# Layer 0's fp8 rounding in a two-layer Flamingo block: scaling on GpSimd, rounding in one ACT and two DVE operations

## The chip, the cores and the metric

The kernel runs on one core of one Trainium2 chip. A core has five engines that run side by side and meet at semaphores: TensorE (PE) for matrix products, VectorE (DVE), ScalarE (ACT) and GpSimd (POOL) for elementwise work, and SyncE (SP), which issues most DMAs. PE writes to PSUM; DVE and ACT read PSUM and SBUF; POOL reads SBUF. The time is that of one execution on the device in microseconds (us), the median of several; the profile is of one further execution.

## What is computed

Two layers of a gated block on x of 4 x 512 x 512, each a cross attention and a feed-forward part, each added to x with a factor tanh(g). The change touches the cross "attention" of layer 0 alone, which is a product of two quantized matrices:

```python
def quant_dequant_act_1x128(x):
    amax = jnp.max(jnp.abs(xb), axis=-1, keepdims=True)      # blocks of 128 along a row
    safe = jnp.maximum(amax, ACT_EPS)
    q = (xb * (FP8_MAX / safe)).astype(jnp.float8_e4m3fn)
    return (q.astype(jnp.float32) * (safe / FP8_MAX)).reshape(E, M, K)
...
xq = quant_dequant_act_1x128(x)           # x is layer-normed
wq = quant_dequant_weight_128x128(weight) # the same with 128 x 128 blocks; weight is the context
return jnp.einsum('emk,enk->emn', xq, wq)
```

So each block is scaled up to the range of an 8-bit float (3 bits of mantissa, the largest value 448), rounded to that format, and scaled down again. Behind it come layer 0's feed-forward part (weights rounded to -1, 0, 1; activations to 8-bit integers; two Gelu in a row), layer 1's attention with 16 heads, and layer 1's mixture of 8 experts.

## The kernel before

All of x lies in SBUF as 16 row tiles of 128 x 512 (`x_sb`). The work is staged: layer 0 (cross product and feed-forward woven together), then layer 1's attention, then the shared and the routed experts, which end with rows added to the output by scattering DMAs (L1481).

Layer 0 is written as steps `step(s)`, s from -7 to 14, each a slice through a pipeline over row tiles t: `cross_rows(s + 7)` normalizes, scales, rounds and scales back one row tile; `cross_product(s + 6)` turns the row tile before it on PE (L754), copies it from PSUM on ACT (L758), multiplies it with the quantized context (L761) and adds the result to `x_sb` on DVE (L768); `row_stats`, `row_norm` and `row_quant` (L797 to L846) prepare the tile for the feed-forward part; `hidden(s)` is its first product (L862) with two Gelu (L870, L877), `hidden_scales` takes the sum of squares on ACT (L885) and the largest value on DVE (L888, a 128x2048 reduction), `hidden_quant` rounds (L902), `down(s - 2)` is the second product (L912). The four contexts (`cross_context(b)`, each 128 x 4 x 512) are prepared in pieces between the steps: key and value products for layer 1 (L669, L681), the largest value of each 128 x 128 block (L696 to L711), and then, for each of the 4 chunks of 512 columns, the scaling up, the rounding and the scaling down. The two weights of the feed-forward part are summed (L637), and rounded on ACT and DVE (L659, L660), in steps -6 to -1.

The quantization before the change:

- Scaling up: for a context chunk, one DVE multiplication of 128x512 with the factors broadcast along 128 columns (L715); for a row tile, four ACT multiplications of 128x128, each with a factor for each row (L741).
- Rounding, `fp8_round`: four DVE operations on 128x512 (L136 to L141). The exponent of each value is cut out, scaled so that adding and subtracting it leaves 3 bits of mantissa, added, and subtracted.
- Scaling down: four ACT multiplications of 128x128 (L722 for a context, L747 for a row tile).

There are 16 context chunks and 16 row tiles, 32 units of 512 columns. POOL in layer 0 does only small operations: the power -1/2 of a few columns (L126, L804, L788), for which DVE waits behind each statistic. In layer 1 POOL adds the exponentials of the attention (L389, 128x1024) and a bias row to x (L1411, 128x512).

Each engine runs its instructions in its own order. That order isn't the source's: a scheduler arranges them by its own model of costs, except where the source pins them. Buffers come from rotating pools: row tiles `v` have 3 buffers, the rounding's scratch `e` has 2.

Of the kernel before, what the change touches and what calls it, by code (L numbers as in the profile page):

```python
# [10 lines left out]
F32 = mybir.dt.float32  # L11
BF16 = mybir.dt.bfloat16
I32 = mybir.dt.int32
I16 = mybir.dt.int16
U8 = mybir.dt.uint8
AF = mybir.ActivationFunctionType
ALU = mybir.AluOpType
# [3 lines left out]
P = 128  # L21
# [3 lines left out]
DC = D // P  # L25
# [18 lines left out]
FP8_MAX = 448.0  # L44
# [4 lines left out]
def flamingo_kernel(  # L49
# [22 lines left out]
    nc = tc.nc  # L72
# [9 lines left out]
    def acc(name):  # L82
        return ps_acc.tile([P, 512], F32, tag="acc", name=name)
# [45 lines left out]
    def layer_norm(dst, t, i, mv, rstd):  # L129
        nc.vector.tensor_scalar(  # L130
            dst, x_sb[:, t, :], mv[:, i, 0:1], rstd[:, i : i + 1], ALU.subtract, ALU.mult
        )

    def fp8_round(y, e):

        nc.vector.tensor_scalar(  # L136
            e.bitcast(I32), y.bitcast(I32), 0x7F800000, None, ALU.bitwise_and
        )
        nc.vector.tensor_scalar(e, e, 2.0**-6, 1.5 * 2.0**20, ALU.max, ALU.mult)
        nc.vector.tensor_tensor(y, y, e, ALU.add)  # L140
        nc.vector.tensor_tensor(y, y, e, ALU.subtract)  # L141

# [414 lines left out]
    with ExitStack() as l0:  # L559
# [9 lines left out]
        with ExitStack() as ph:  # L569
            other = ExitStack()  # L570
            cpool = other.enter_context(tc.tile_pool(name="cpool", bufs=3, side="right"))
            apool = other.enter_context(tc.tile_pool(name="apool", bufs=2, side="right"))
# [90 lines left out]
            def cross_context(b):  # L663


                c = state["ctx", b]
                k_ps = acc(f"k_ps_{b}")
                for dc in range(DC):
                    nc.tensor.matmul(  # L669
                        k_ps,  # L670
                        lhsT=wk_sb[:, dc, :],
                        rhs=c[:, dc, :],
                        start=dc == 0,
                        stop=dc == DC - 1,
                    )
                nc.scalar.copy(kT[:, b, :], k_ps)
                yield
                v_ps = acc(f"v_ps_{b}")
                for kc in range(TB):
                    for dc in range(DC):  # L680
                        nc.tensor.matmul(  # L681
                            v_ps[:, kc * P : (kc + 1) * P],
                            lhsT=c[:, dc, kc * P : (kc + 1) * P],
                            rhs=wv_sb[:, dc, :],
                            start=dc == 0,
                            stop=dc == DC - 1,
                        )
                nc.scalar.copy(
                    v_sb[:, b * TB : (b + 1) * TB, :], v_ps.rearrange("p (c n) -> p c n", c=TB)
                )  # L690
                yield
                cb = c.rearrange("p c (n q) -> p (c n) q", q=P)

                am = small.tile([P, 16], F32, tag="cam", name=f"cam_{b}", bufs=2)
                for ns in [slice(4 * dc, 4 * dc + 4) for dc in range(DC)] if b == 0 else [slice(16)]:
                    nc.vector.tensor_reduce(  # L696
                        am[:, ns], cb[:, ns, :], AX.X, ALU.max, apply_absolute_value=True
                    )
                tp = acc(f"tpm_{b}")
                nc.tensor.transpose(tp[:16, :P], am, ident)  # L700
                peak = small.tile([16, 1], F32, tag="cpeak", name=f"cpeak_{b}", bufs=2)
                nc.vector.tensor_reduce(peak, tp[:16, :P], AX.X, ALU.max)
                wide = small.tile([16, P], F32, tag="cwide", name=f"cwide_{b}", bufs=2)
                nc.vector.tensor_copy(wide, peak.to_broadcast([16, P]))
                nc.tensor.transpose(tp[:, P : P + 16], wide, ident[:16, :16])
                safe = small.tile([P, 16], F32, tag="csafe", name=f"csafe_{b}", bufs=2)
                nc.vector.tensor_scalar_max(safe, tp[:, P : P + 16], 1e-6)
                up = small.tile([P, 16], F32, tag="cup", name=f"cup_{b}", bufs=2)
                nc.vector.reciprocal(up, safe)
                nc.vector.tensor_scalar_mul(up, up, FP8_MAX)  # L710
                nc.vector.tensor_scalar_mul(safe, safe, 1.0 / FP8_MAX)  # L711
                yield
                for dc in range(DC):
                    ns = slice(dc * 4, dc * 4 + 4)
                    nc.vector.tensor_tensor(  # L715
                        cb[:, ns, :], cb[:, ns, :], up[:, ns].unsqueeze(2).to_broadcast([P, 4, P]),
                        ALU.mult,
                    )
                    e = apool.tile([P, 512], F32, tag="e", name=f"ce_{b}_{dc}")
                    fp8_round(c[:, dc, :], e)  # L720
                    for n in range(dc * 4, dc * 4 + 4):
                        nc.scalar.mul(cb[:, n, :], cb[:, n, :], safe[:, n : n + 1])  # L722
                    yield

            def cross_stats(b):
# [2 lines left out]
            def cross_rows(t):  # L728

                v = apool.tile([P, D], F32, tag="v", name=f"va_{t}", bufs=3)  # L730
                layer_norm(v, t, t % TB, *state["a", t // TB])
                vb = v.rearrange("p (c q) -> p c q", q=P)
                am = small.tile([P, DC], F32, tag="xam", name=f"xam_{t}")
                nc.vector.tensor_reduce(am, vb, AX.X, ALU.max, apply_absolute_value=True)
                nc.vector.tensor_scalar_max(am, am, 1e-4)
                up = small.tile([P, DC], F32, tag="xup", name=f"xup_{t}")
                nc.vector.reciprocal(up, am)
                nc.vector.tensor_scalar_mul(up, up, FP8_MAX)
                nc.vector.tensor_scalar_mul(am, am, 1.0 / FP8_MAX)
                for dc in range(DC):  # L740
                    nc.scalar.mul(vb[:, dc, :], vb[:, dc, :], up[:, dc : dc + 1])  # L741
                state["va", t] = v
                yield
                e = apool.tile([P, 512], F32, tag="e", name=f"xe_{t}")
                fp8_round(v, e)
                for dc in range(DC):
                    nc.scalar.mul(vb[:, dc, :], vb[:, dc, :], am[:, dc : dc + 1])  # L747
                yield

            def cross_product(t):  # L750
# [210 lines left out]
            with ExitStack() as first:  # L961
                stg = first.enter_context(tc.tile_pool(name="stg", bufs=4))
                ws = (w1T, w2T)
                wd = (w1q, w2q)
                load_batch(1)
                load_rows(1)
                load_weight(stg, 0, ws[0])
                load_batch(2)
                for b in range(2, B):
                    load_rows(b)  # L970
                go(cross_context(0), 7)
                cross_stats(0)

                def w(f, k, *cs):
                    return [lambda c=c: f(k, c, wd[k]) for c in cs]

                ctx1, ctx2 = cross_context(1), cross_context(2)
                step(-7)
                step(-6, [lambda: go(ctx1, 2)] + w(weight_sum, 0, 0, 1))
                step(-5, [lambda: go(ctx1, 2)] + w(weight_sum, 0, 2, 3))  # L980
                weight_mean(0)
                scales_left(0)
                step(-4, [lambda: go(ctx1, 3), lambda: cross_stats(1)] + w(weight_round, 0, 0, 1))
                load_weight(stg, 1, ws[1])
                step(-3, w(weight_round, 0, 2, 3) + w(weight_sum, 1, 0))
                load_batch(3)
                step(-2, [lambda: go(ctx2, 2)] + w(weight_sum, 1, 1, 2, 3))
                weight_mean(1)
                scales_left(1)
                step(-1, [lambda: go(ctx2, 2)] + w(weight_round, 1, 0, 1, 2, 3))  # L990
            hpool = ph.enter_context(tc.tile_pool(name="hpool", bufs=2))
            state["hpool"] = hpool
            step(0, [lambda: go(ctx2, 3), lambda: cross_stats(2)])
            ctx3 = cross_context(3)
            step(1)
            step(2, [lambda: go(ctx3, 3)])
# [292 lines left out]
    def rt(name, last=E, dtype=F32):  # L1289
        return dpool.tile([P, NT, last], dtype, name=name)  # L1290
# [17 lines left out]
    for n in range(2):  # L1308
        m, f = rt(f"m{n}", 1), rt(f"f{n}", 1)
# [285 lines left out]
```

## Time and profile before

| | us |
|---|---|
| median of 3 runs | 1294.44 (1291.94 to 1295.09) |
| the profiled execution | 1293.68, its span 1291.9 |
| PE busy over the span | 1188.1 (92%) |
| DVE busy | 610.2 (47%) |
| ACT busy | 511.2 (40%) |
| POOL busy | 410.7 (32%) |
| first and last Gelu on a product (L870) | start at 103.2 and 302.0 |
| first rounding (L136), last scaling down (L747) | start at 23.8 and 226.2 |

The granted clock of PE is 0.964 of full speed on average. In the profile a group is given by its line in the kernel, engine, operation, output and inputs with their shapes, count, busy time in us and the mean duration of one in ns; behind the bar stands the idle time of the engine just before these instructions and who ended it. Busy time of neighbours that overlap is counted once. In timelines a line has the start in us, the time of the merged pieces, and in brackets the idle time ahead of it.

### The profile page before, as it was taken

The numbers are of one execution on the slowest core, as the hardware profiler recorded it, in microseconds if no ns is written. First come the engines' busy times: TensorE is split into PE (matmuls) and PEld (weight loads), VectorE is DVE, ScalarE is ACT, GpSimd is POOL, SyncE is SP. The second block draws the span as 40 slices with busy tenths as digits, with TensorE's granted clock in tenths as the row PEclk, the third lists the DMA queues.
The fourth block names the chain that finished last, engine by engine and source line by source line (L and its number), as shares of the span: only waits on it lengthen the run. The fifth ranks groups of instructions, "written<-read, shape, count | busy, mean of one in ns | idle before, by whom it ended". The sixth has DMA issues, their size and how long they took to land. (4 is left out here: it accounts for less than half of the span.)

```text
span 1291.9 us, 14505 instructions
## 1 busy us (share of the span) xinstructions
PE 1188.1 (92%) x5354; PEld 550.2 (43%) x5354; DVE 610.2 (47%) x1160; ACT 511.2 (40%) x709; POOL 410.7 (32%) x408
## 2 busy tenths in 40 slices
PE   3776798899799999999999999999999999999995
PEld 1432343344233333333333554544335555555553
DVE  8789999688456666656654301331121111111110
ACT  4688898686355544444552110200001221211221
POOL 1000100101277877767686201136100111111111
PEclk8888999899899999999999889999999999999998
DMA  9230232335021211111003000027315886888782
GB/s 355 75 112 9 41 62 42 86 79 116 25 67 34 66 35 38 63 34 58 2 1 146 2 1 1 1 82 278 98 66 164 251 248 191 262 258 255 206 249 33
DMA packets 88753, 135.33 MB, mean 105 GB/s; under 512 B 52836, under 2 KB 54120, under 8 KB 84840
## 3 DMA queue, kind: packets, MB, share of 16 engines
q1 hardware_dynamic: 80936, 116.52, 28.3%
q0 software_dynamic: 7744, 17.86, 6.4%
q8 instruction: 43, 0.70, 0.2%
q14 instruction: 30, 0.25, 0.1%
HBM read 113.84 MB, written 32.32 MB: 113 GB/s over the span
## 5 line engine op out<-in xcount | busy, mean ns | idle before, releaser
L428 ACT ACTIVATE ex<-s,mbias,mk 128x1024 f32<-128x1024 f32 x128 | 147.2, 1200 | 140.7 <-PE s L239 140.7
L319 DVE TENSOR_REDUCE nmax<-s 128x2 f32<-128x1024 f32 x128 | 150.2, 1215 | 98.6 <-PE s L239 87.9
L1445 PE MATMUL gue<-w,xT 128*128 128x352 f32 x576 | 176.1, 459 | 0.0
L1481 POOL DMA_INDIRECT out_dram<-ye,row_i x36 | 55.5, 1541 | 320.1 <-ACT ye L1480 216.5
L389 POOL TENSOR_TENSOR part<-part,ex 128x1024 f32<-128x1024 f32 x62 | 144.6, 2354 | 16.3 <-PE sm L239 11.4
L1202 PE MATMUL gu<-xnT_d,w 128*128 128x512 f32 x320 | 144.0, 610 | 0.0
L1445 PEld LDWEIGHTS gue<-w,xT 128*128 128x128 f32 x576 | 109.2, 190 | 70.5 <-issue 16.9
L1465 DVE COPY hT<-tph_e 128x256 f32<-128x256 f32 x36 | 15.3, 425 | 255.2 <-PE tph_e L1463 255.2
L1472 PE MATMUL oe<-w,hT 128*128 128x512 f32 (+1 forms) x216 | 102.4, 610 | 3.8 <-ACT ye L1480 0.6
L1202 PEld LDWEIGHTS gu<-xnT_d,w 128*128 128x128 f32 x320 | 62.5, 196 | 78.3 <-issue 78.3
L761 PE MATMUL oa<-ctx,vTa 128*128 128x512 f32 x128 | 67.4, 675 | 18.9 <-ACT vTa L758 18.9
L1191 ACT ACTIVATE sg<-gu,sgb 128x512 f32<-128x512 f32 x20 | 13.7, 687 | 178.5 <-PE gu L1202 178.5
L389 POOL TENSOR_TENSOR part<-ex,ex 128x1024 f32<-128x1024 f32 x32 | 75.8, 2388 | 23.1 <-ACT ex L428 23.0
L912 PE MATMUL ob<-w2q,hqT 128*128 128x512 bf16 x256 | 64.9, 407 | 13.5 <-DVE hqT L838 10.3
L1453 ACT ACTIVATE sge<-gue 128x352 f32<-128x352 f32 x36 | 16.7, 463 | 151.5 <-PE gue L1445 151.5
L239 PE MATMUL s<-row_tables 10*128 10x512 bf16 (+1 forms) x512 | 67.5, 383 | 9.1 <-DVE nmax L319 5.7
L239 PE MATMUL s<-k,qT 32*128 32x512 f32 x512 | 72.2, 604 | 0.4 <-ACT qT L287 0.4
L239 PE MATMUL s<-qT,k 32*128 32x512 f32 x512 | 71.6, 598 | 0.0
L1192 DVE SCALAR_TENSOR_TENSOR hd<-gu,sub,sg 128x512 f32<-128x512 f32 x20 | 15.0, 751 | 117.9 <-ACT sg L1191 117.9
L239 PE MATMUL av<-ex,kv 128*32 128x512 f32 x512 | 69.2, 605 | 0.4 <-ACT ex L428 0.4
L239 PE MATMUL q_ps<-xnT,wq_sb 128*128 128x512 f32 (+1 forms) x156 | 68.8, 553 | 0.0
L239 PE MATMUL oc<-wo,attnT 128*128 128x512 f32 (+1 forms) x164 | 66.3, 525 | 0.0
(257 smaller groups left out, 1684.0 us busy)
## 6 DMA issues: line engine op xcount, KB each, us to landing
w<-in_e_w_dram SPq DMA_DIRECT2D x36, 1408.0 KB
w<-in_e_w_dram SPq DMA_DIRECT2D x36, 768.0 KB
slots<-row_tables SPq DMA_DIRECT2D x13, 771.0 KB
xr<-slots SPq DMA_DIRECT2D x36, 256.0 KB
stage<-in_w1T_dram SPq DMA_DIRECT2D x4, 1024.0 KB
stage<-in_w2T_dram SPq DMA_DIRECT2D x4, 1024.0 KB
k<-kv SPq DMA_DIRECT2D x64, 64.0 KB
out_dram<-x_sb SPq DMA_DIRECT2D x16, 256.0 KB
```

The lines of the kernel that those rows point to most:

```text
L239: tc.keep_in_program_order(nc.tensor.matmul(*args, **how))
L319: largest = nc.vector.tensor_reduce(nmax[:, i, 2 * j : 2 * j + 2], sc[j], AX.X, ALU.max, negate=True)
L389: nc.gpsimd.tensor_tensor(part[:, hs, :], old[:, hs, :], ex[:, hs, :], ALU.add)
L428: nc.scalar.activation(ex[:, 2 * j : 2 * j + 2, :], sc[j], AF.Exp, bias=mbias[:, b, kc : kc + 1], scale=mk[:, b, kc : kc + 1],)
L761: nc.tensor.matmul(o_ps[:, 0, :], lhsT=vT[:, dc, :], rhs=cq[:, dc, :], start=dc == 0, stop=dc == DC - 1,)
L912: nc.tensor.matmul(o_ps, lhsT=hqT[:, c, :], rhs=w2q[:, c * D : (c + 1) * D], start=c == 0, stop=c == IC - 1,)
L1202: nc.tensor.matmul(gu[:, m, :], lhsT=w[:, dc, c * P : (c + 1) * P], rhs=xnT[:, dc, b * S : (b + 1) * S], start=dc == 0, stop=dc == DC - 1,)
L1445: nc.tensor.matmul(gu[:, m, :I], lhsT=xT[:, dc, :], rhs=wt[:, dc, :], start=dc == 0, stop=dc == DC - 1,)
L1453: nc.scalar.activation(sg, gu[:, 0, :I], AF.Silu)
L1465: nc.vector.tensor_copy(hT[:, :2, :], tp[:, : 2 * P].rearrange("p (c q) -> p c q", q=P))
L1472: nc.tensor.matmul(o_ps[:, 0, :], lhsT=hT[:ni, c, :], rhs=dw[:ni, c, :], start=c == 0, stop=c == len(ICH) - 1,)
L1481: added = nc.gpsimd.indirect_dma_start(out=out, out_offset=bass.IndirectOffsetOnAxis(ap=row_i[:, j, 0:1].bitcast(I32), axis=0), in_=y, in_ ...
```

## The change

The scaling of a unit, up or down, is one POOL multiplication of 128x512 with the factors broadcast along 128 columns, for contexts and row tiles alike; the rounding is one ACT operation that writes the scaled absolute value as bf16, and two DVE operations with two tensors each, which leave the negated rounded value; the factor that scales back is negative accordingly. The scratch `e` becomes bf16.

```diff
+    def scale_blocks(y, by):
+        nc.gpsimd.tensor_tensor(y, y, by.unsqueeze(2).to_broadcast([P, 4, P]), ALU.mult)
+
     def fp8_round(y, e):
-        nc.vector.tensor_scalar(
-            e.bitcast(I32), y.bitcast(I32), 0x7F800000, None, ALU.bitwise_and
-        )
-        nc.vector.tensor_scalar(e, e, 2.0**-6, 1.5 * 2.0**20, ALU.max, ALU.mult)
-        nc.vector.tensor_tensor(y, y, e, ALU.add)
-        nc.vector.tensor_tensor(y, y, e, ALU.subtract)
+        least = 1.5 * 2.0**14
+        nc.scalar.activation(e, y, AF.Abs, scale=2.0**20)
+        nc.vector.scalar_tensor_tensor(y, e, least, y, ALU.max, ALU.add)
+        nc.vector.scalar_tensor_tensor(y, e, least, y, ALU.max, ALU.subtract)
...
-                nc.vector.tensor_scalar_mul(safe, safe, 1.0 / FP8_MAX)
+                nc.vector.tensor_scalar_mul(safe, safe, -1.0 / FP8_MAX)
...
-                    nc.vector.tensor_tensor(
-                        cb[:, ns, :], cb[:, ns, :], up[:, ns].unsqueeze(2).to_broadcast([P, 4, P]),
-                        ALU.mult,
-                    )
-                    e = apool.tile([P, 512], F32, tag="e", name=f"ce_{b}_{dc}")
+                    scale_blocks(cb[:, ns, :], up[:, ns])
+                    e = apool.tile([P, 512], BF16, tag="e", name=f"ce_{b}_{dc}")
                     fp8_round(c[:, dc, :], e)
-                    for n in range(dc * 4, dc * 4 + 4):
-                        nc.scalar.mul(cb[:, n, :], cb[:, n, :], safe[:, n : n + 1])
+                    scale_blocks(cb[:, ns, :], safe[:, ns])
...
-                nc.vector.tensor_scalar_mul(am, am, 1.0 / FP8_MAX)
-                for dc in range(DC):
-                    nc.scalar.mul(vb[:, dc, :], vb[:, dc, :], up[:, dc : dc + 1])
+                nc.vector.tensor_scalar_mul(am, am, -1.0 / FP8_MAX)
+                scale_blocks(vb, up)
...
-                e = apool.tile([P, 512], F32, tag="e", name=f"xe_{t}")
+                e = apool.tile([P, 512], BF16, tag="e", name=f"xe_{t}")
                 fp8_round(v, e)
-                for dc in range(DC):
-                    nc.scalar.mul(vb[:, dc, :], vb[:, dc, :], am[:, dc : dc + 1])
+                scale_blocks(vb, am)
```

## The prediction

> **What bounds the kernel now.** I read the busy slices first, then a table of stretches, then the groups and timelines of the first 240 us. The 40 slices are 32.3 us each.
>
> ```profile
> PE   3776798899799999999999999999999999999995
> ...
> DVE  8789999688456666656654301331121111111110
> ACT  4688898686355544444552110200001221211221
> POOL 1000100101277877767686201136100111111111
> ```
>
> Layer 0 is slices 1 to 10. There DVE is the fullest engine (7 to 9 tenths), ACT close behind, PE seldom full, and POOL almost empty. From slice 11 on PE is full. The chain of waits ends in the scatter of the last stage and goes back only to 1040 us, so it says nothing of layer 0; but attention needs layer 0's result and PE is full from there on, so what layer 0 gains or loses moves the end by as much.
>
> ```profile
> 20.00:40.00 20.00, 4.43 (x14) 2.14 (x13) 19.65 (x46) 16.05 (x34) 1.02 (x1) 0.57 0.74 278
> 40.00:60.00 20.00, 18.37 (x70) 10.35 (x70) 11.75 (x37) 9.76 (x19) 0.00 (x0) 0.92 0.03 7
> 60.00:80.00 20.00, 13.04 (x29) 5.47 (x28) 18.10 (x45) 19.03 (x40) 1.01 (x1) 0.83 0.71 256
> ...
> 100.00:120.00 20.00, 13.55 (x41) 5.85 (x40) 19.94 (x49) 17.46 (x38) 1.55 (x2) 0.83 0.07 14
> ...
> 160.00:180.00 20.00, 19.94 (x82) 9.03 (x81) 19.04 (x59) 20.00 (x35) 1.14 (x2) 1.00 0.33 62
> ```
>
> Columns: stretch, its length, busy time of PE, weight loads, DVE, ACT, POOL, the granted clock, DMA. DVE works over 18 of 20 us nearly everywhere; only 40 to 60 us waits on PE (18.37). Over 20 to 240 us DVE is busy 192.6 of 220 us (0.88), ACT 178. From 160 us PE and ACT are full too: a cheaper DVE would soon meet them there.
>
> **DVE, removed and added.** Per unit of 512 columns (16 context units, 16 row tiles) four roundings go, and per context unit the up-scaling.
>
> ```profile
> L140 DVE TENSOR_TENSOR va<-va,xe 128x512 f32<-128x512 f32 x16 | 10.8, 682 | 0.0
> ...
> L715 DVE TENSOR_TENSOR ctx<-ctx,cup 128x512 f32<-128x512 f32 x16 | 10.5, 683 | 0.0
> ...
> L139 DVE TENSOR_SCALAR xe<-xe 128x512 f32<-128x512 f32 x16 | 6.6, 418 | 0.0
> ...
> L212 DVE SCALAR_TENSOR_TENSOR ali<-ali,part,ali 128x512 f32<-128x512 bf16 x2 | 1.5, 748 | 0.0
> ```
>
> Neighbours overlap by some 0.08 us (in the timeline two L141 together take 1.28 us, two L139 0.75), so one costs 0.60 and 0.33 us of DVE. Removed: 32 x (0.33 + 0.33 + 0.60 + 0.60) + 16 x 0.60 = 69.1 us. Added: 64 scalar_tensor_tensor with a bf16 and an f32 input. L212 is that form, 748 ns, less 0.08: 64 x 0.67 = 42.9 us. Net -26.2 us.
>
> **ACT.** 192 scalings of 128x128 go; their three groups (L722, L741, L747) are busy 20.1 + 20.2 + 20.4 = 60.7 us. 32 Abs of 512 columns to bf16 come: L148, a bf16 cast of the same size, takes 618 ns, 0.52 with the overlap: 16.6 us. Net -44.1 us. No table load is added in the built order: the first and the Gelu table each stay in for all their Abs.
>
> **POOL.** 64 multiplications of 128x512 come. Its one row of that size is below. The second factor is broadcast along the inner axis, which no row shows; I take 1.27 us; the bounds are half of L389's 128x1024 (2.35 us), 1.18, and four of L414's 128x128 (0.456 us), 1.82, if each block of the broadcast were started anew. 64 x 1.27 = 81 us, onto the 19 us that POOL is busy up to 240 us. POOL is no bound by that alone. What counts is whom it stops.
>
> ```profile
> L1411 POOL TENSOR_TENSOR x_sb<-x_sb,sdb x16: 1260/1265/1498, 723.1 to 857.2; 128x512 f32<-128x512 f32 x16
> ```
> ```profile
> L130 DVE TENSOR_SCALAR vc<-x_sb,mv_c,rstd_c x16: 527/548/1993, 251.2 to 480.9; 128x512 f32<-128x512 f32 x16
> L130 DVE TENSOR_SCALAR vx<-x_sb,mv_d,rstd_d x16: 532/542/1490, 708.7 to 724.8; 128x512 f32<-128x512 f32 x16
> ```
> ```profile
> 368.85 1.98 DVE L130 TENSOR_SCALAR vc<-x_sb,mv_c,rstd_c 128x512 f32<-128x512 f32 x1 [2.49 <-PE tp L262]
> ```
> ```profile
> 368.20 4.84 POOL L389 TENSOR_TENSOR part<-ex,ex 128x1024 f32<-128x1024 f32 x2 [4.65 <-ACT ex L428]
> ```
> ```profile
> 822.18 1.26 DVE L1317 SCALAR_TENSOR_TENSOR prob<-hot,prob 128x128 f32<-128x128 f32 x1
> ```
> ```profile
> 822.02 1.26 POOL L1411 TENSOR_TENSOR x_sb<-x_sb,sdb 128x512 f32<-128x512 f32 x1 [2.18 <-DVE x_sb L1243]
> ```
>
> The reader is to see that DVE and POOL block each other. L130 takes 0.54 us alone, and up to 1.99 us when a POOL tensor_tensor is running: it starts at 368.85, the first of two POOL instructions (2.35 us each) ends at 370.55, and DVE ends 0.28 us later. A scalar_tensor_tensor with both inputs in SBUF does the same: 1.26 us instead of the 0.29 of its neighbours, ending 0.14 us behind POOL's end. DVE instructions that read PSUM, and reductions, run on (L319 stays at 1.2 us under POOL's 2.35). In layer 0 the changed kernel puts 64 POOL instructions beside just the kinds that are stopped: the 64 new two-input ones, L130 (0.54) and L838 (0.28 and 0.68).
>
> A DVE instruction that meets a 1.27 us POOL instruction at its start loses some 0.97 us (1.26 - 0.29), later in it less. In the built order of a row tile the up-scaling starts while DVE has the 2.28 us reduction L888 or the reduction L734 before it: nothing lost. The down-scaling starts right behind the second new instruction, and what follows on DVE is L130, L838 or the next unit's pair: nearly all of 0.97. In a context block four units are dense and the two engines alternate. So 0.5 us for each of the 64: +32 us of DVE; bounds 0 and 0.97 (0 and +62).
>
> The Trainium skill, "SBUF — State Buffer", section "Who interferes with whom", says that the two share one port pair as an exclusive lock held for the whole instruction, against 2-port modes and two SBUF inputs. By that sentence taken at its worst, each multiplication stopping DVE for its full length, DVE's change would be -26 + 81 = +55 us; the rows above show a DVE instruction slipping in between two queued POOL instructions, and the sum goes by them.
>
> **What else moves.** The rounding's chain becomes POOL (1.27), ACT (0.62), DVE, POOL, where it was DVE alone up to the last step. At the first context (22.6 us) nothing else is ready for DVE: it stands for 1.27 + 0.62 + 0.1 = +2 us (at the other three, rows in work cover it; bounds 0 and 8). Behind the multiplications stand POOL's 28 small pow instructions (L126, L788, L804), and DVE waits for these already now, 11.3 us in all (5.0 + 2.7 + 2.4 + 1.2). POOL is then busy some 0.4 of the time, so a pow finds on average 0.4 x 0.63 = 0.25 us ahead of it, 7 us in all; I put half on DVE's path: +3.5 (bounds 0 and 28 x 1.27 = 36). ACT's relief counts where ACT was last: between 56 and 82 us it is full, and 28 scalings (8.9 us) give way to some 7 Abs (3.6), so the second weight's sums come 5 us sooner, less the 2 to 3 us by which the first row tile is late: -3 (bounds 0 and -5.5). DMA issues on SP stand in the same order.
>
> **The sum.** DVE's own change, -26.2 + 32 = +5.8, counts at DVE's share 0.88: +5. With +2, +3.5 and -3 it is +7.5. The profiled execution took 1293.68 us (span 1291.9), 0.8 below the median of 1294.44. 1293.7 + 7.5 = 1301 us. With 0.25 us lost per POOL instruction, nothing else lost and ACT's full relief: (-26.2 + 16) x 0.88 - 5.5 = -14.5, 1279 us. With 0.75 us, and 4 and 7 for the waits: (-26.2 + 48) x 0.88 + 11 = +30, 1324 us.
>
> **Rivals.**
> 1. Faster: the scheduler's order lets the multiplications fall beside reductions and PSUM reads, which POOL does not stop. For it: L888 (36 us in all), L734, L815, L121 and L797 are a large part of DVE's time. Against it: the down-scaling starts right behind the pair. Place: DVE, 20 to 240 us; it decides below 0.35 us lost per multiplication (26.2 x 0.88 = 23.1, less 2.5 of the other terms, over 64 x 0.88), and over 0.3% faster needs 0.29. At 0.25 us and the middle of the other terms, -9 + 2.5 = -6.5 to -14.5: about 1283 us. 0.28.
> 2. No change: the gains of ACT and the losses of DVE cancel, as PE paces the steps from 160 us on (19.94 of 20): 1294 us. 0.17.
> 3. Much slower: POOL and DVE alternate all through layer 0, 0.97 us each time, which POOL at 1.82 us would also bring: (-26.2 + 62) x 0.88 + 2.5 = +34, 1328 us. 0.10.
> 4. It does not do what it says: Abs would need a table beside Gelu's. Each of some 17 Abs after 100 us would cost two loads of 1.28 us (44 us), but the built order has none. 0.02, with the slower ones.
>
> **How the numbers follow.** My forecast, 1301 us with its own range 1294 to 1312, has 0.43. 0.3% (3.9 us) is about what a measurement can tell from no change. Faster by more: rival 1, 0.28, and a little of the rest, 0.29. Within: rival 2 and the lower end of the forecast, 0.17. Slower: 0.54. The range 1280 to 1324 takes in rivals 1 and 2 and leaves most of 3 and 4 out.
>
> **What would show it.** Right: the new DVE pair's mean well over 0.75 us (near 1.1), L130's and L838's means in layer 0 grown from 0.54 and 0.68, POOL some 100 us busy up to 240 us, DVE's busy time about what it was, first Gelu (103.2 us now) at 101 to 107. Wrong: the pair at 0.75 us, L130 unchanged, and the last Gelu (300.4 us now) sooner.

## The result, and the profile after

The changed kernel takes 1305.58 us (median of 4, 1304.37 to 1306.84) beside 1293.61 us for the kernel before: ratio 1.0093, 95% interval 1.0075 to 1.0111. The profiled execution has a span of 1302.6 us, 10.7 more than before. The first Gelu on a product starts at 109.1 us (before 103.2), the last at 308.9 (302.0): layer 0 is 6.9 us longer. The remaining 3.8 us lie behind it, in code that the change does not touch.

The busy slices of the changed kernel (32.6 us each):

```profile
PE   2767888799899999999999999998999999999995
...
DVE  7798888788556666666654401331122111111110
ACT  3357666677255554544453210100001112112221
POOL 4444441111268777767686201146000111111111
```

In layer 0 (the first ten digits) POOL has gone from almost nothing to four tenths in the first six slices, ACT has fallen by up to three tenths, and DVE is less full than before in five of the ten. The same in stretches (PE, weight loads, DVE, ACT, POOL, granted clock, DMA):

```profile
20.00:40.00 20.00, 1.52 (x11) 1.14 (x10) 17.18 (x30) 12.53 (x16) 13.57 (x11) 0.65 0.77 291
40.00:60.00 20.00, 18.28 (x72) 10.40 (x71) 10.90 (x30) 3.44 (x6) 4.90 (x5) 0.93 0.00 1
60.00:80.00 20.00, 11.70 (x20) 4.51 (x18) 19.70 (x28) 15.22 (x16) 11.63 (x11) 0.75 0.62 216
100.00:120.00 20.00, 14.94 (x42) 6.45 (x42) 16.16 (x33) 12.83 (x12) 9.41 (x8) 0.81 0.04 7
160.00:180.00 20.00, 14.10 (x53) 6.32 (x53) 17.51 (x35) 14.01 (x15) 10.16 (x8) 0.91 0.32 59
```

At 20 to 40 us DVE has 17.18 us of work where it had 19.65, and at 160 to 180 us PE has 14.10 where it had 19.94. PE has as much to do at 40 to 60 us as before (18.28), and DVE is full at 60 to 80 us; in the other three stretches no engine is full, and everybody waits for somebody. The groups of the new DVE pair, up to 310 us (busy, then the mean in ns):

```profile
L145 DVE SCALAR_TENSOR_TENSOR ctx<-ce,ctx 128x512 f32<-128x512 bf16 x16 | 16.4, 1037 | 2.2 <-ACT ce L144 2.0
L145 DVE SCALAR_TENSOR_TENSOR va<-xe,va 128x512 f32<-128x512 bf16 x16 | 14.8, 930 | 0.7 <-ACT xe L144 0.6
L146 DVE SCALAR_TENSOR_TENSOR ctx<-ce,ctx 128x512 f32<-128x512 bf16 x16 | 12.0, 770 | 0.0
...
L146 DVE SCALAR_TENSOR_TENSOR va<-xe,va 128x512 f32<-128x512 bf16 x16 | 11.3, 709 | 0.0
```

And two of the four groups of multiplications, from the view of one line (shortest, median, longest in ns):

```profile
L136 POOL TENSOR_TENSOR va<-va,xup x16: 1040/1041/1482, 15.6 to 218.7; 128x512 f32<-128x512 f32 x16
...
L136 POOL TENSOR_TENSOR ctx<-ctx,csafe x16: 1036/1357/2171, 29.8 to 177.4; 128x512 f32<-128x512 f32 x16
```

A multiplication takes 1.04 us where DVE leaves it alone, and up to 2.17 us where it does not. How the two meet is seen in the first context, first DVE, then POOL:

```profile
25.94 0.85 DVE L145 SCALAR_TENSOR_TENSOR ctx<-ce,ctx 128x512 f32<-128x512 bf16 x1 [1.81 <-ACT ce L144]
26.94 1.30 DVE L145 SCALAR_TENSOR_TENSOR ctx<-ce,ctx 128x512 f32<-128x512 bf16 x1
28.16 2.13 DVE L146 SCALAR_TENSOR_TENSOR ctx<-ce,ctx 128x512 f32<-128x512 bf16 x2
30.52 2.66 DVE L145 SCALAR_TENSOR_TENSOR ctx<-ce,ctx 128x512 f32<-128x512 bf16 x2 [0.23 <-ACT ce L144]
```
```profile
24.20 4.94 POOL L136 TENSOR_TENSOR ctx<-ctx,cup 128x512 f32<-128x512 f32 x4
29.83 2.80 POOL L136 TENSOR_TENSOR ctx<-ctx,csafe 128x512 f32<-128x512 f32 x2 [0.69 <-DVE ctx L146]
33.93 2.80 POOL L136 TENSOR_TENSOR ctx<-ctx,csafe 128x512 f32<-128x512 f32 x2 [1.29 <-DVE ctx L146]
```

POOL's four up-scalings run from 24.20 to 29.14. The second chunk's L145 waits for the end of one of them (1.30 in place of 0.68), two L146 take 2.13 in place of 1.28, and when the down-scalings start at 29.83 two L145 take 2.66.

### The profile page after: what moved, and what is told of

It reads as the page before. It is cut to its first block, busy times and chain, and to the rows that moved or that the text cites. A ratio compares the mean times of both kernels' runs of the same rounds, so it can differ in the third digit from the quotient of the medians.

```text
span 1302.6 us, 14354 instructions
## 1 busy us (share of the span) xinstructions
PE 1185.9 (91%) x5338; PEld 548.8 (42%) x5354; DVE 605.2 (46%) x1080; ACT 472.9 (36%) x549; POOL 488.9 (38%) x472
## 5 line engine op out<-in xcount | busy, mean ns | idle before, releaser
L394 POOL TENSOR_TENSOR part<-part,ex 128x1024 f32<-128x1024 f32 x62 | 144.6, 2355 | 16.5 <-PE sm L244 11.4
L1201 PEld LDWEIGHTS gu<-xnT_d,w 128*128 128x128 f32 x320 | 62.2, 196 | 77.7 <-issue 77.7
L760 PE MATMUL oa<-ctx,vTa 128*128 128x512 f32 x128 | 72.0, 715 | 15.5 <-ACT vTa L757 15.5
```

The lines of the kernel that those rows point to most:

```text
L394: nc.gpsimd.tensor_tensor(part[:, hs, :], old[:, hs, :], ex[:, hs, :], ALU.add)
L760: nc.tensor.matmul(o_ps[:, 0, :], lhsT=vT[:, dc, :], rhs=cq[:, dc, :], start=dc == 0, stop=dc == DC - 1,)
L1201: nc.tensor.matmul(gu[:, m, :], lhsT=w[:, dc, c * P : (c + 1) * P], rhs=xnT[:, dc, b * S : (b + 1) * S], start=dc == 0, stop=dc == DC - 1,)
```

## The experiments

Twelve kernels in three groups of four; each is compared with the kernel before on the chip that its group ran on. To read them I split layer 0 by DVE's time: its busy time up to the start of the last Gelu, and its idle time from 20 us on, summed by the engine that ended each wait. The two add up to the last Gelu but for 7 to 9 us at the start. The line numbers of the variants differ by a few.

| kernel | DVE busy | DVE idle | of it on ACT | on POOL | last Gelu | ratio to before |
|---|---|---|---|---|---|---|
| before | 259.5 | 35.2 | 5.8 | 11.2 | 302.0 | |
| before, again | 259.3 | 35.1 | 6.7 | 11.4 | 301.4 | 0.9993 (0.9971 to 1.0015) |
| changed | 254.9 | 46.0 | 9.3 | 18.5 | 308.9 | 1.0093 (1.0075 to 1.0111) |
| changed, again | 254.9 | 48.2 | 9.4 | 18.5 | 311.3 | 1.0066 (1.0045 to 1.0086) |
| round_alone | 243.0 | 52.9 | 22.5 | 12.4 | 305.1 | 1.0022 (1.0002 to 1.0042) |
| scale_alone | 280.7 | 33.3 | 5.0 | 15.6 | 321.4 | 1.0165 (1.0130 to 1.0201) |
| scale_dve | 265.0 | 34.5 | 8.7 | 10.0 | 306.9 | 1.0048 (1.0021 to 1.0076) |
| beside | 301.6 | 36.6 | 6.1 | 12.6 | 345.6 | 1.0334 (1.0293 to 1.0375) |
| no_round | 204.5 | 57.1 | 24.2 | 14.1 | 270.1 | 0.9765 (0.9722 to 0.9807) |
| scratch4 | 257.1 | 38.7 | 8.5 | 14.5 | 304.4 | 0.9986 (0.9967 to 1.0006) |
| round_four | 242.7 | 62.2 | 25.4 | 11.9 | 313.9 | 1.0076 (1.0043 to 1.0109) |
| up_pool_four | 245.2 | 62.9 | 23.0 | 15.0 | 316.1 | 1.0164 (1.0138 to 1.0191) |
| rowup_pool_four | 246.0 | 52.4 | 18.5 | 12.4 | 306.7 | 1.0054 (1.0026 to 1.0082) |
| ctxdown_pool_four | 249.4 | 38.1 | 9.1 | 14.6 | 295.7 | 0.9932 (0.9900 to 0.9963) |

A slower PE does not explain the change: up to the last Gelu its granted clock is 0.91 before and 0.90 in the changed kernel, and DVE's waits for PE are 17.1 and 15.9 us. The waits that grew most, in the kernel before and then in the changed one:

```profile
DVE ham L893 <- POOL nc_h L788: 4.3, 9, 0.7
```
```profile
DVE ham L892 <- POOL nc_h L787: 6.9, 9, 2.4
DVE va L130 <- POOL rstd_a L126: 3.8, 2, 1.9
```

Both are DVE standing for a small power of POOL (total, times, longest, in us).

**The rounding alone.** `fp8_round` of the changed kernel, scalings of the kernel before:

```diff
-                    scale_blocks(cb[:, ns, :], safe[:, ns])
+                    for n in range(dc * 4, dc * 4 + 4):
+                        nc.scalar.mul(cb[:, n, :], cb[:, n, :], safe[:, n : n + 1])
...
-                scale_blocks(vb, up)
+                for dc in range(DC):
+                    nc.scalar.mul(vb[:, dc, :], vb[:, dc, :], up[:, dc : dc + 1])
```

> The new rounding (one ACT, two DVE operations) with the scalings of the kernel before (contexts: up on DVE, down on ACT; rows: both on ACT); POOL multiplies nothing. Theory L (POOL's multiplications stop DVE, the new rounding by itself is a gain): DVE loses 32 x (0.33 + 0.33 + 0.60 + 0.60) = 59.5 us and gets 42.9, at the share of 0.88 that is -14.6 us; ACT gets 32 Abs of 0.52 us, some 8 of them where ACT is full, +4: 1283 us (1278 to 1290), the pair's mean at 0.68 us. Rival Q (what costs is the hop from engine to engine and the wait in another engine's queue, not the blocking): the Abs stands behind ACT's long Gelu, DVE idles for it, and the time is 1294 to 1302 us with DVE's busy time down by 16 us and its idle time up by as much.

Theory L is refuted as to the time: without a single POOL multiplication the kernel is no faster than before (1.0022). DVE's busy time fell by 16.5 us, as both expected, and its idle time rose by 17.7, of which 16.7 is waiting for ACT. Q's picture holds. The pair is at its own price, from the view of its first line:

```profile
L145 DVE SCALAR_TENSOR_TENSOR ctx<-ce,ctx x16: 680/684/692, 25.0 to 181.8; 128x512 f32<-128x512 bf16 x16
L145 DVE SCALAR_TENSOR_TENSOR va<-xe,va x16: 671/682/691, 35.2 to 229.1; 128x512 f32<-128x512 bf16 x16
```

No instance is over 0.69 us; in the changed kernel the same instruction reaches 1.52. So all of the stretching there is POOL's.

**The scaling alone.** The four DVE operations of the kernel before between POOL's multiplications:

```diff
-        nc.scalar.activation(e, y, AF.Abs, scale=2.0**20)
-        nc.vector.scalar_tensor_tensor(y, e, least, y, ALU.max, ALU.add)
...
+        nc.vector.tensor_tensor(y, y, e, ALU.add)
+        nc.vector.tensor_tensor(y, y, e, ALU.subtract)
```

> The scalings on POOL as in the changed kernel, the rounding by the four DVE operations of the kernel before. L: DVE loses only the 16 up-scalings of contexts (9.6 us) and is stopped by POOL 64 times for about 0.37 us, 24 us: (24 - 9.6) x 0.88 = +12.7, less up to 5 for ACT's relief of 60.7 us: 1301 to 1308 us, and DVE's operations behind a down-scaling are longer than in the kernel before. Q: the chain of a unit has as many hops as before (POOL, DVE, POOL for ACT, DVE, ACT), so what counts is the work taken off: -9.6 x 0.88 = -8.4, 1283 to 1290 us.

L's side, and more than it said: DVE is busy 21.2 us longer although 9.6 us of work were taken from it, so 30.8 us are lost to POOL, 0.48 for each multiplication, and layer 0 grows by 19.4 us. ACT's relief (its scalings of 60.7 us) bought next to nothing: DVE's idle time fell by 1.9 us.

**The scaling on DVE.** One word differs from the changed kernel:

```diff
-        nc.gpsimd.tensor_tensor(y, y, by.unsqueeze(2).to_broadcast([P, 4, P]), ALU.mult)
+        nc.vector.tensor_tensor(y, y, by.unsqueeze(2).to_broadcast([P, 4, P]), ALU.mult)
```

> The changed kernel with the 64 multiplications on DVE in place of POOL: same instructions, same number, no POOL. DVE gets 64 x 0.60 = 38.4 us, so that against the kernel before it has +12.2 us and ACT -44 us. L: without POOL the pair costs 0.68 us each and nothing is stretched: +12.2 x 0.88 = +10.7, less up to 5 for ACT: 1299 to 1306 us, so that DVE doing the work itself costs about what POOL's doing it beside DVE costs. Q: with two hops fewer in the chain it is clearly better than the changed kernel: under 1298 us.

L's numbers (1.0048 of 1294 is 1300), though the lower end of the interval, 1297, reaches into Q's. DVE's busy time rose by 5.5 us, not by 12.2. DVE doing all 64 multiplications itself is no worse for layer 0 (last Gelu 306.9) than POOL doing them (308.9 and 311.3).

**The multiplications beside the old kernel.**

```diff
+            def beside(by):
+                nc.gpsimd.tensor_tensor(
+                    idle, idle, by.unsqueeze(2).to_broadcast([P, 4, P]), ALU.mult
+                )
...
+                    beside(up[:, ns])
...
+                    beside(safe[:, ns])
...
+                beside(up)
...
+                beside(am)
```

> The kernel before with 64 POOL multiplications of 128x512 (second factor broadcast) added, on a tile of their own that nobody reads; each starts when the factors of a unit are there, nothing waits for it but POOL's own later work. L: they stop DVE as in the changed kernel, 64 x 0.37 = 24 us, at 0.88 +21: 1305 to 1322 us, with DVE's busy time up by 15 us or more. Q: nothing hangs on them: 1292 to 1298 us.

Here Q is refuted, and L's price was too low: +43.5 us in layer 0, DVE busy 42.1 us longer, 0.66 us for each multiplication that nobody waits for. The first context in the kernel before, and here, DVE and then POOL:

```profile
23.82 0.75 DVE L136 TENSOR_SCALAR ce<-ctx 128x512 int32<-128x512 int32 x2
24.49 0.75 DVE L139 TENSOR_SCALAR ce<-ce 128x512 f32<-128x512 f32 x2
```

```profile
24.99 2.44 DVE L136 TENSOR_SCALAR ce<-ctx 128x512 int32<-128x512 int32 x2
27.34 2.44 DVE L139 TENSOR_SCALAR ce<-ce 128x512 f32<-128x512 f32 x2
29.70 2.97 DVE L140 TENSOR_TENSOR ctx<-ctx,ce 128x512 f32<-128x512 f32 x2
```
```profile
26.04 1.10 POOL L669 TENSOR_TENSOR row_tables<-row_tables,cup 128x512 f32<-128x512 f32 x1
27.22 1.10 POOL L669 TENSOR_TENSOR row_tables<-row_tables,csafe 128x512 f32<-128x512 f32 x1
28.39 1.10 POOL L669 TENSOR_TENSOR row_tables<-row_tables,cup 128x512 f32<-128x512 f32 x1
29.57 1.10 POOL L669 TENSOR_TENSOR row_tables<-row_tables,csafe 128x512 f32<-128x512 f32 x1
```

The two engines take turns: one POOL instruction every 1.18 us, one DVE instruction between two of them. The one-tensor operations L136 and L139 are stopped as well as the two-tensor ones (0.75 us for two in the kernel before, 2.44 here). So each theory holds for a part: POOL's multiplications stop DVE, as L says, and what the new rounding takes off DVE comes back as waiting for ACT (`round_alone`), as Q says.

**Both kernels once more.**

> The kernel before once more, unchanged, for a second profile. In the five other profiles the stretch from the last Gelu to the end takes 993.7 to 996.3 us, in the first one of this kernel 989.8. Theory P (the change costs only inside layer 0, 6.9 us by the last Gelu; what follows differs by chance): layer 0 as before (first Gelu 103, last 302 us), the rest 993 to 997 us, and a span of 1295 to 1299 us. Rival R (the changed kernels also slow what follows layer 0): the rest is 989 to 991 us again.

> The changed kernel once more, unchanged. P: first Gelu at 109 and last at 309 us again (within 1 us), the rest 990 to 997 us, and a ratio to the kernel before of 1.004 to 1.008, less than the 1.009 of the first comparison if that held 4 us of chance. R: the rest at 994 us again beside 990 of the kernel before, ratio 1.008 to 1.010.

Layer 0 of the kernel before repeats (103.2 and 301.4). The stretch behind the last Gelu does not: 984.5 us beside 989.9, lower than either theory said. The changed kernel has 985.9 beside 993.7, and over all the profiles of the study, with the same code there, it lies between 983.9 and 996.3. So the 3.8 us behind layer 0 in the first pair of profiles are not shown to be the change's, and nothing here supports R. In layer 0 the changed kernel is 6.9 and 9.9 us behind; P's figures for the Gelu, 109 and 309, were missed by some 2 us (111.2 and 311.3).

**What DVE's time is worth.** All of `fp8_round` is left out of the kernel before.

> The kernel before without its rounding: the four DVE operations of all 32 units are left out (59.5 us of DVE), the scalings stay. It asks what DVE's time in layer 0 is worth at all. As the prediction counted it (DVE's time at 0.88): -52 us, last Gelu at 250 us, 1240 to 1250 us. P (from the first Gelu on the other engines set the pace, 198.8 us from first to last with 16 us less of DVE in the kernel with the rounding alone): from first to last Gelu 185 to 199 us, only the start is shorter (by some 5 to 10 us): last Gelu at 280 to 297 us, 1272 to 1290 us.

Between the two: 55 us of DVE removed bring the last Gelu 31.9 us forward, 0.58 of what is removed. First to last Gelu is 185.6 us, as P said, but the start gains 18.7 us, more than P's 5 to 10. DVE then waits 24.2 us for ACT.

**Four scratch buffers.** The Abs on ACT writes `e`, and frees nothing until DVE has done the pair. In the changed kernel, ACT's idle time in front of the Abs line:

```profile
  DVE va L146: 6.8, 2
  DVE ctx L146: 4.8, 4
```

11.6 us of waiting for a buffer. What it does is seen at the end of the last context, on ACT, DVE and PE:

```profile
164.93 0.63 ACT L144 ACTIVATE ce<-ctx 128x512 bf16<-128x512 f32 x1
...
172.59 0.63 ACT L144 ACTIVATE ce<-ctx 128x512 bf16<-128x512 f32 x1 [2.70 <-DVE hqs L894]
```
```profile
174.51 0.68 DVE L145 SCALAR_TENSOR_TENSOR ctx<-ce,ctx 128x512 f32<-128x512 bf16 x1
175.11 1.52 DVE L837 TENSOR_SCALAR hqT<-hqT 128x2048 bf16<-128x2048 int16 x1
```
```profile
176.69 3.44 PE L911 MATMUL ob<-w2q,hqT 128*128 128x512 bf16 x9 [5.85 <-DVE hqT L837]
```

The last two Abs of this context stand 7.7 us apart, since the second has its buffer only when L146 of a row tile ends at 172.48 (the bracket names DVE's next instruction, which ended 0.1 us later). So its pair comes late on DVE, and the conversion of hqT (the rounded hidden tile, an input of PE's second product), which DVE has in order behind it, meets POOL's down-scaling (174.73 to 176.08) and takes 1.52 us in place of 0.68. PE stands 5.85 us for it.

```diff
-                    e = apool.tile([P, 512], BF16, tag="e", name=f"ce_{b}_{dc}")
+                    e = apool.tile([P, 512], BF16, tag="e", name=f"ce_{b}_{dc}", bufs=4)
```

(and the same for `xe`)

> The changed kernel with four buffers for the scratch e in place of two (in bf16 they take the room of the two in f32). In the first context of the changed kernel the third Abs waits 2 us for a buffer while POOL has scaled up all four chunks. If it is the hand-over between the engines that delays layer 0's start, the first Gelu comes 2 to 5 us sooner than at 109.1 and the time is 1298 to 1303 us; if it is POOL's blocking of DVE (the pair's mean stays at 0.9 to 1.04 us), no change: within 2 us of the changed kernel.

It is 0.8% faster than the changed kernel in the same group (0.9986 to 1.0066), better than either case said. At the place above, ACT and PE now:

```profile
163.74 1.14 ACT L144 ACTIVATE ce<-ctx 128x512 bf16<-128x512 f32 x2
```
```profile
172.99 2.55 PE L911 MATMUL ob<-w2q,hqT 128*128 128x512 bf16 x11 [2.56 <-DVE hqT L837]
```

The two Abs run one behind the other, the conversion takes 0.68 us again, and PE waits 2.56 us. The wait in front of the Abs falls from 12.7 us (the changed kernel's second profile) to 3.6, DVE's idle time by 9.5 and the last Gelu by 6.9 us. The place was not where I expected it: the first Gelu comes 0.9 us sooner than at 109.1 (2.9 sooner than in the second profile), the rest is won later. POOL's stops are untouched (L145 on a context has a mean of 1.07 us, 1.04 in the changed kernel, and reaches 1.52 in both). With four buffers the change is in its time no longer slower than the kernel before (0.9986), though layer 0 still ends 2.4 to 3.0 us later in this profile: DVE's work is 2.4 us less, its waits are 3.5 us more, and the rest is at the start. One thing is not separated: with four buffers DVE's instructions also stand in another order (the two profiles of the changed kernel have one and the same), and what that order alone is worth was not tried.

**Which part of the scaling POOL can take.** Four variants with four buffers; the edits exchange single `scale_blocks` calls for the operations of the kernel before, as above.

> The new rounding alone (scalings as in the kernel before, none on POOL), now with four scratch buffers. With two it was 1.0022 of the kernel before. Theory H (with two buffers an Abs waits at the head of ACT's queue until DVE has done a pair, and Gelu, PE's copies and the 8-bit rounding stand behind it): ratio 0.990 to 0.998, last Gelu at 296 to 301 us. Rival A (ACT's 16 us of added work is what eats the gain: ACT is busy 244 us up to the last Gelu, as much as DVE): 1.000 to 1.005 again, last Gelu at 302 to 306 us.

H falls here: with POOL out, no Abs had waited for a buffer (1.2 us of idle time in front of the line), so two more could free nothing; they only gave another order of instructions, 8.7 us worse at the last Gelu. Rival A fits better, though the loss is larger than it said (1.0076 and 313.9, beyond its 1.005 and 306). DVE's waits in this kernel:

```profile
DVE ham L893 <- ACT h L882: 11.8, 5, 5.6
DVE nc_h L790 <- ACT hq L890: 10.6, 7, 4.3
```

Both are DVE standing for ACT's 2048-column operations on the hidden tile (3.8 and 2.0 us in the kernel before).

> The new rounding with four scratch buffers; POOL scales up (32 multiplications), ACT scales down (contexts and rows). DVE up to the last Gelu: 243 (rounding alone) - 9.6 + 32 x 0.37 = 245 us, ACT 244 - 20 = 224 us. If what counts is the load of DVE and ACT and the hand-over: 0.988 to 0.996 of the kernel before. If every POOL multiplication costs its 0.37 us and a place in the chain as well: 0.996 to 1.003.

> The new rounding with four scratch buffers; POOL scales the contexts down (16 multiplications), the rest as in the kernel before (contexts up on DVE, rows on ACT). DVE: 243 + 16 x 0.37 = 249 us, ACT 244 - 20 = 224 us. If load counts: 0.990 to 0.997, and better than the rounding alone by what ACT is relieved (rival A); if POOL's stops count more: no better than the rounding alone.

> The new rounding with four scratch buffers; POOL scales the row tiles up (16 multiplications), the rest as in the kernel before. Same loads as with the contexts' down-scaling on POOL (DVE 249, ACT 224 us), but the multiplication stands behind four small DVE operations, which run on while POOL works only if no operation of two tensors follows: 0.988 to 0.996 if load counts, 0.997 or more if the hop from DVE to POOL to ACT in the row's chain counts.

Three kernels with almost the same loads (DVE 245, 249 and 246 us, ACT 227 to 228) lie 2.3% apart, so load alone settles nothing. `up_pool_four` is slower than both of its ranges, `rowup_pool_four` is in its second, `ctxdown_pool_four` in its first. What separates them most in the table is DVE's wait for ACT: 23.0 and 18.5 us where ACT still scales the contexts down, 9.1 where POOL does (its waits for PE go the same way, 22.3, 18.1 and 13.0). That holds for the new rounding throughout: 22.5 and 25.4 in the two kernels with it alone, 8.5 to 9.4 where contexts are scaled down by POOL or DVE. `ctxdown_pool_four` is faster than the kernel before and the changed one:

```profile
20.00:40.00 20.00, 6.16 (x19) 2.83 (x18) 19.55 (x35) 14.98 (x29) 8.45 (x5) 0.66 0.77 292
60.00:80.00 20.00, 17.21 (x44) 7.68 (x43) 18.56 (x35) 17.05 (x25) 6.21 (x5) 0.83 0.72 252
160.00:180.00 20.00, 18.64 (x75) 8.57 (x74) 18.92 (x63) 18.28 (x28) 3.83 (x4) 1.00 0.18 34
```
```profile
L136 POOL TENSOR_TENSOR ctx<-ctx,csafe x16: 1037/1363/3170, 26.8 to 166.7; 128x512 f32<-128x512 f32 x16
```

DVE is as full as before (19.55, 18.56, 18.92 us), while PE already has 17.21 us at 60 to 80 us where it had 13.04. Nobody waits soon for a context that is scaled down, so POOL's slowness (up to 3.17 us for one multiplication) stays hidden. That this placing and not the order that came with it is the cause has not been separated.

## Why the prediction was right in its time, and where its steps were wrong

**Direction and size.** 1301 was forecast and 1305.6 measured, but the sum came out through two errors that cancel, which is luck. It said DVE +5.8 us and waits +2.5. Measured up to the last Gelu: DVE -4.6, its waits +10.8.

**POOL's price.** "I take 1.27 us" was wrong for a multiplication alone, and the lower bound of 1.18 too: it takes 1.04 us. Beside DVE, which stops POOL as well, the 64 have a mean of 1.21, so that POOL's busy time up to 240 us, put at some 100 us, came to 97.

**DVE's pair.** Priced at 0.67 us from L212; alone it is 0.68 with the overlap still in it (0.748 for L212), so 64 x 0.07 = 4 us cheaper in all. Beside POOL L145 came to 0.93 and 1.04, near the 1.1 that was named as the sign, L146 only to 0.71 and 0.77; the mean of all 64 is 0.86.

**Blocking.** The mechanism was right and is shown: `beside` adds it alone, and where `round_alone` and `scale_dve` take it away no L145 takes more than 0.69 us. The size, "0.5 us for each of the 64", was too high in the changed kernel: DVE should have lost 26.2 us, or 30 by the pair's true price, and lost 4.6, so POOL cost it 22 to 26 us, 0.34 to 0.40 each. (Added up over the instructions that stood longer than their own price beside a multiplication, it is 24 us, 0.37 each.) In `scale_alone` it is 0.48 and in `beside` 0.66: the price hangs on how dense DVE is when the multiplication comes. L130 and L838 (L837 now) hardly grew: means of 0.62 and 0.59 from 0.54, and 0.75 from 0.68.

**The rule of the Trainium skill.** "SBUF — State Buffer", section "Who interferes with whom", calls the shared pair an exclusive lock; `beside` agrees with it, with one POOL and one DVE instruction in turn. Taken at its worst it would have given +55 us of DVE for the changed kernel; the trace has -4.6, since of the 77 us that the 64 multiplications took DVE lost only 22 to 26.

**"DVE's own change counts at DVE's share 0.88".** This is the step that failed. DVE time that is added counts in full (`beside`: +42.1 busy, +43.5 in layer 0; `scale_alone`: +21.2 and +19.4). DVE time that is taken away counts at 0.58 (`no_round`) or not at all (`round_alone`: -16.5 and +3.1, where ACT also has the Abs to do), because DVE then waits for ACT: 24.2 and 22.5 us of waiting, 5.8 in the kernel before.

**The waits.** The first context's +2 was right (1.81 in front of the first L145). The delay of POOL's small powers was put at +3.5 and is +7.3 (DVE's idle time on POOL 11.2 to 18.5; nc_h alone 4.3 to 6.9). ACT's relief was put at -3, with the second weight's sums 5 us sooner; the operation that gives its scale started 6.6 us later (89.9 to 96.5), as all before it was late. The wait for a scratch buffer, 11.6 us on ACT with all of ACT's queue behind it, was not in the sum: I named what stands behind POOL's queue, and not what stands behind the Abs in ACT's.

**Rivals.** The first (multiplications fall beside reductions) was close in its number (it decides below 0.35, which by its own terms, 20.6 over 56.3, is 0.37), and still wrong in its sign, for DVE's gain did not count. The second was right that another engine would set the pace, but that was ACT and the hand-over rather than PE. The third is nearest to `beside` (0.66, not 0.97), not to this kernel. No table load came with Abs (six in both profiles).

**Signs.** First Gelu at 109.1, beyond the 101 to 107 named. The "last Gelu (300.4 us now)" is the last but one; the last started at 302.0.

## What to carry to other kernels

Split the fullest engine's time into busy and waiting, by whom: here work added to an engine that is 0.88 full cost its whole length, and of work taken off it four tenths or all came back, as waiting for the next engine above all. A second engine that stops the first, as POOL stops DVE, seems a place for work that nobody waits for soon rather than for links of a chain: with four buffers, 16 multiplications moved so gave -0.7%, all 64 -0.1%. When one engine's operation becomes a chain over three, count the buffers between them first (all 64 with two buffers: +0.7 to +0.9%).

## What the runs showed of the hardware

- A POOL multiplication of 128x512 f32 whose second factor is broadcast along the inner axis takes 1.04 us alone; an addition of two full tensors takes 1.26 (L1411).
- DVE operations of 128x4 on one tensor can be stopped as well: L739 took 1.02 us in place of 0.16 when it met POOL's multiplication; L895, of 128x1, was not stretched (0.215 us at most).
- In some executions signals of PE come late behind layer 0, while DMAs scatter rows (L1394 in the changed kernel). Two profiles of the changed kernel, the same ACT instruction:

```profile
889.77 0.69 ACT L1190 ACTIVATE sg_h<-gu_h,sgb 128x512 f32<-128x512 f32 x1 [14.91 <-remote]
```
```profile
883.52 0.69 ACT L1190 ACTIVATE sg_h<-gu_h,sgb 128x512 f32<-128x512 f32 x1 [6.28 <-PE gu_h L1217]
```

In the first, PE's last product for it ended at 881.1 us, its signal came 8.66 us later, together with those of two later products, and PE then stood for 5.5 us. Such a delay (8 to 16 us for the first signal held up) is in the profiles of all eight kernels of the first and third groups and in none of the four of the second, the kernel before and the changed one among these. It does not account for the spread of 984 to 996 us by itself: `ctxdown_pool_four` has it, and the shortest stretch. What causes it was not tried.
